# Values by heads copied from SBUF, odd heads' partition halves exchanged, and the output's bank moved

## The chip, the cores and the metric

The kernel runs on one core of one Trainium2 chip. The metric is the time of one execution on the device in microseconds (us); lower is better. Before the change the median of three runs is 4178.27 us (4174.99 to 4178.63).

TensorE (PE in the profile, PEld for its weight loads) multiplies into PSUM, an accumulator memory of eight banks; a bank holds 128 partitions of 512 fp32 values. VectorE (DVE), ScalarE (ACT) and GpSimd (POOL) do the element-wise work. Large data lives in the chip's main memory and comes through SBUF, the on-chip memory, by DMA.

## The reference, cut to what matters

The input is 16 images of 64 x 64 positions with 128 channels. Layer 0 is a two-dimensional LSTM over the grid. Layer 1 is Nystrom attention with 8 heads of 16 channels over the 4096 tokens of an image, followed by a recurrent network. The change is in the attention:

```python
q_l = q.reshape(b, h, m, l, dh).mean(axis=3)      # 64 landmarks
k_l = k.reshape(b, h, m, l, dh).mean(axis=3)
attn1 = softmax(q @ k_l^T);  attn2 = softmax(q_l @ k_l^T);  attn3 = softmax(q_l @ k^T)
out = attn1 @ pinv(attn2) @ (attn3 @ v)
res = conv(v, conv_w)        # 33 taps along the tokens, one filter per head
out = (out + res) @ w_out + b_out
```

What is concerned is `res`, the convolution of the values along the token axis, and the buffers around it. A tile holds 128 tokens, so that a 33-tap filter needs 16 tokens of the tile before and 16 of the tile after.

## The kernel before

The program does group statistics, the LSTM grid, the landmarks and the pseudo-inverse, then `attention` (from about 1760 to 3880 us of the profile's span), then `recurrence`.

In `attention` an image is 32 tiles of 128 tokens, and four tiles make a group of 512 tokens: Q = 8 groups per image, 128 in all. The loop at the end of the function runs 145 steps. A step `s` is `b, q = divmod(s, 8)`, and it works on five groups at once, each at another stage: `new` (group s: queries, keys and values are projected), `mid` (group s-8: weights of the landmarks over the keys), `nxt` (s-15: queries against landmarks, for their maxima), `cur` (s-16: softmax over landmarks and output) and `prev` (s-17: normalisation and the feed to the next layer). Beside them each step does an eighth of the convolution of an earlier image: one pair of heads, over one half (16 tiles) of that image. In the steps q = 0 to 3 it is the second half of image b-2, in q = 4 to 7 the first half of image b-1; 128 such pieces in all.

Inside `tc.manual_schedule` the order on every compute engine is the order of the program text, written out by hand in `step`. The framework puts in the semaphores. It lets no two engines touch one PSUM bank of a tile at the same time, reads included.

PSUM's banks are given by number (`bank(k, shape)`), and a new tile in a bank waits until the readers of the old one have finished. The uses in a step that matter here, in order:

- Banks 0 to 3: `soften(cur)`; then 0, 1, 2 for keys, queries and values in `project(new)`; then 0 to 3 for `greatest(new)`, the key scores of four head pairs, whose maxima DVE takes.
- Banks 4 to 7: `compare(nxt)`, then `weigh(mid)`, then 4 and 5 for `attend(cur)`: the denominators (`gr.den`) and the numerators. Bank 6 then takes `values(mid)` and, later in the step, `output(cur)`. Bank 4 takes the turned convolution in `add_convolved(cur)`. Bank 5 takes `feed(prev)`. Bank 7 takes the convolution.
- `gather(mid)`, once per image at the end of the step q = 7, uses bank 4.

The values of a group come out in bank 2 of `project`. ACT copies them into SBUF (`gr.V`, line 747), and DVE copies them once more out of the same bank into `im.VH`, where they lie by heads (line 749). `im.VH` is what the convolution streams.

`convolve` (line 848) multiplies a head's band matrix, 128 x 128, with the 256 columns (16 tiles x 16 channels) of that head's values: the products inside a tile. `convolve_edges` (line 860) adds the products with the neighbouring tiles. They are small, 32 rows by 32 output tokens: the last 32 tokens of the tile before act on the first 32 of a tile, the first 32 of the tile after on its last 32. Each pair of heads has four of them, all in bank 7. Both heads of a pair use the same rows of TensorE's array: rows 96 to 127 for the one side and 0 to 31 for the other. ACT then copies the bank to `R` (line 864).

In the step q = 3 (`early`) the convolution is done inside `project`, in bank 3 and ahead of the copy at line 749, since that copy writes a tile of `VH` that the convolution of the older image still reads. In all other steps `convolve` stands after `values(mid)` and `convolve_edges` at the end of the step.

`conv_bands` fills the band and edge matrices once, before the loop.

## Time and profile before

| | us |
|---|---|
| median of the runs | 4178.27 |
| profiled execution, its own time | 4171.5 |
| its span, first to last instruction | 4170.0 |
| PE busy | 3949.4 (95%) |
| DVE busy | 2952.6 (71%) |
| POOL busy | 2786.3 (67%) |
| ACT busy | 2521.7 (60%) |
| one image in the middle of `attention` (8 steps) | 125.55 |
| one plain step there | 15.46 |

The profile's page gives each engine's busy time, the chain of work that ended last, and groups of instructions by source line. The timeline lists instructions by start and merges like ones: start, duration of the merged piece, engine, line, operation, names, shape and count, and in square brackets how long the engine stood idle before it and what ended that. An fp32 product of TensorE is two matmul instructions, so counts of matmuls are twice those in the text of the program.

### The profile page before, as it was taken

The numbers are of one execution on the slowest core, as the hardware profiler recorded it, in microseconds if no ns is written. First come the engines' busy times: TensorE is split into PE (matmuls) and PEld (weight loads), VectorE is DVE, ScalarE is ACT, GpSimd is POOL, SyncE is SP. The second block draws the span as 40 slices with busy tenths as digits, with TensorE's granted clock in tenths as the row PEclk, the third lists the DMA queues.
The fourth block names the chain that finished last, engine by engine and source line by source line (L and its number), as shares of the span: only waits on it lengthen the run. The fifth ranks groups of instructions, "written<-read, shape, count | busy, mean of one in ns | idle before, by whom it ended". The sixth has DMA issues, their size and how long they took to land.

```text
span 4170.0 us, 99395 instructions
## 1 busy us (share of the span) xinstructions
PE 3949.4 (95%) x37750; PEld 2661.1 (64%) x37750; DVE 2952.6 (71%) x7136; ACT 2521.7 (60%) x4925; POOL 2786.3 (67%) x4183
## 2 busy tenths in 40 slices
PE   7999999999999979689999999999999999988697
PEld 5857655555676768546666666666666666655386
DVE  8678777777777854346777777777777777757565
ACT  0566655555665643246666766666666666655597
POOL 0677777777777743127788787787787787777133
PEclk9899999999999979899999999999999999989798
DMA  8223322233332200212333333323333323223699
GB/s 330 55 66 82 81 74 78 79 81 82 81 83 73 74 18 4 62 31 61 89 88 83 91 87 84 92 82 89 90 82 89 91 80 91 80 66 86 226 261 182
DMA packets 497778, 386.33 MB, mean 93 GB/s; under 512 B 40464, under 2 KB 470416, under 8 KB 494992
## 3 DMA queue, kind: packets, MB, share of 16 engines
q1 hardware_dynamic: 479888, 346.35, 28.6%
q0 software_dynamic: 17408, 33.56, 4.5%
q8 instruction: 301, 4.93, 0.5%
q14 instruction: 181, 1.48, 0.1%
HBM read 173.74 MB, written 206.18 MB: 91 GB/s over the span
## 4 chain that ended last, share of the span: by engine, by line
PE 85%; DVE 6%; ACT 3%; issue 2%; DMA 2%; POOL 2%; SPq 0%; DVEq 0%; POOLq 0%; ACTq 0%
PE ls_z L194 14%; PE ls_z L198 13%; PE at_bank L737 3%; PE at_bank L775 3%; PE at_bank L848 3%; PE at_bank L860 3%; PE at_bank L982 3%; PE at_bank L809 3%; PE at_bank L745 3%; PE at_bank L930 3%; PE at_bank L954 3%; PE at_bank L740 3%; PE at_bank L887 3%; PE at_bank L920 3%; PE at_bank L824 2%; PE at_bank L721 2%
## 5 line engine op out<-in xcount | busy, mean ns | idle before, releaser
L200 ACT ACTIVATE ls_g<-ls_z,ls_b 128x304 f32<-128x304 f32 (+26 forms) x950 | 509.3, 548 | 369.8 <-PE ls_z L198 333.4
L839 POOL TENSOR_TENSOR at_total<-at_total,at_e 128x512 f32<-128x512 f32 x480 | 612.3, 1276 | 131.5 <-ACT at_e L815 102.6
L194 PE MATMUL ls_z<-ls_xn,ls_w 128*128 128x304 f32 (+26 forms) x1900 | 610.2, 469 | 8.2 <-DMA ls_w<-in_L_conv_wf_dram 5.1
L194 PEld LDWEIGHTS ls_z<-ls_xn,ls_w 128*128 128x128 f32 x1900 | 340.8, 196 | 184.5 <-issue 83.9
L711 POOL TENSOR_SCALAR at_T<-at_T,at_nb 128x128 f32<-128x128 f32 x512 | 405.3, 800 | 13.3
L778 DVE TENSOR_REDUCE at_mxq<-at_bank 128x1 f32<-128x512 f32 x512 | 328.5, 683 | 112.9 <-PE at_bank L775 112.7
L198 PE MATMUL ls_z<-ls_hsum,ls_u 128*128 128x304 f32 (+26 forms) x1140 | 371.1, 462 | 0.0
L280 POOL TENSOR_TENSOR ls_g<-ls_g,ls_cell 128x304 f32<-128x304 f32 (+26 forms) x190 | 176.1, 927 | 277.8 <-ACT ls_g L200 264.8
L894 DVE TENSOR_REDUCE at_cmx<-at_bank 128x8 f32<-128x512 f32 x512 | 317.5, 683 | 58.2 <-PE at_bank L887 57.7
L815 ACT ACTIVATE at_e<-at_bank 128x512 f32<-128x512 f32 x512 | 264.4, 602 | 115.6 <-PE at_bank L809 113.1
L923 ACT ACTIVATE at_eT<-at_bank 128x512 f32<-128x512 f32 x512 | 264.4, 602 | 94.4 <-PE at_bank L920 94.4
L198 PEld LDWEIGHTS ls_z<-ls_hsum,ls_u 128*128 128x128 f32 x1140 | 213.3, 196 | 128.6 <-issue 78.2
L237 ACT ACTIVATE ls_tt<-ls_tt,ls_nb 128x128 f32<-128x128 f32 (+9 forms) x632 | 261.0, 478 | 4.1 <-POOL ls_nb L232 4.1
L198 PE MATMUL ls_z<-ls_h,ls_u 128*128 128x304 f32 (+26 forms) x760 | 259.6, 465 | 2.3 <-DVE ls_h L288 2.0
L228 POOL TENSOR_TENSOR ls_tt<-ls_ve,mhalf 128x4 f32<-128x4 f32 (+2 forms) x190 | 228.6, 1203 | 15.2
L281 DVE TENSOR_TENSOR ls_g<-ls_g,ls_g 128x304 f32<-128x304 f32 (+26 forms) x190 | 98.4, 518 | 194.6 <-POOL ls_g L280 193.4
L1192 DVE SCALAR_TENSOR_TENSOR rc_y<-rc_w,rc_scale,rc_z 128x256 f32<-128x256 f32 x344 | 155.3, 480 | 107.6 <-PE rc_z L1179 99.7
L1179 PE MATMUL rc_z<-rc_y,rc_vT 128*128 128x256 f32 x688 | 187.0, 408 | 39.0 <-ACT rc_y L1200 28.1
L749 DVE COPY at_vh<-at_bank 128x512 f32<-128x512 f32 x128 | 88.5, 692 | 184.4 <-ACT at_v L747 153.1
L975 ACT ACTIVATE at_z<-at_u,at_nb,at_r 128x128 f32<-128x128 f32 x512 | 211.7, 505 | 11.2 <-POOL at_nb L970 11.2
L229 POOL TENSOR_TENSOR ls_tt<-ls_ve,mhalf 128x4 f32<-128x4 f32 (+2 forms) x190 | 214.7, 1130 | 0.0
L985 ACT COPY at_fx<-at_bank 128x512 f32<-128x512 f32 x128 | 132.9, 1038 | 127.1 <-DVE wx_stats L983 101.5
(247 smaller groups left out, 9632.2 us busy)
## 6 DMA issues: line engine op xcount, KB each, us to landing
t<-ls_tt SPq DMA_DIRECT2D x392, 130.0 KB
at_T<-t SPq DMA_DIRECT2D x128, 264.0 KB
gs_xb<-in_x_dram SPq DMA_DIRECT2D x16, 2048.0 KB
at_xh<-t SPq DMA_DIRECT2D x128, 256.0 KB
t<-at_u SPq DMA_DIRECT2D x128, 256.0 KB
out_dram<-at_u SPq DMA_DIRECT2D x128, 256.0 KB
wx<-at_fx SPq DMA_DIRECT2D x128, 256.0 KB
rc_w<-wx SPq DMA_DIRECT2D x64, 512.0 KB
```

The source lines that it names most:

```text
L194: nc.tensor.matmul(v.z[g][:, : v.cols], wt[g], v.xn, start=True, stop=False)
L198: nc.tensor.matmul(view(v, v.z[g]), ut[g], hin, start=False, stop=True)
L200: nc.scalar.activation(a[:, : v.cols], v.z[g][:, : v.cols], AF.Tanh if g == 4 else AF.Sigmoid, bias=bt[g])
L228: nc.gpsimd.tensor_tensor(v.tt[:, 0:k, F + 2], ve[:, 0, :k], mhalf[:, :k], ALU.pow)
L229: nc.gpsimd.tensor_tensor(v.tt[:, 0:k, F + 3], ve[:, 1, :k], mhalf[:, :k], ALU.pow)
L237: nc.scalar.activation(v.tt[:q, k, F + 4 :], v.tt[:q, k, 0:F], AF.Identity, bias=v.nb[:q, k : k + 1], scale=v.tt[:q, k, F + 3 : F + 4],)
L711: nc.gpsimd.tensor_scalar(x[:, c, :], x[:, c, :], gr.nbt[:, 0, c : c + 1], gr.nbt[:, 1, c : c + 1], ALU.mult, ALU.subtract)
L778: nc.vector.tensor_reduce(gr.im.mxq[:, n : n + 1, gr.g], gr.s[n], AX.X, ALU.max)
L815: nc.scalar.activation(gr.e[:, n].rearrange("p c m -> p (c m)"), s[n], AF.Exp)
L839: nc.gpsimd.tensor_tensor(total, total, e[:, :, c, :], ALU.add)
L894: nc.vector.tensor_reduce(gr.mx[:, n].rearrange("p j c -> p c j"), gr.s[n].rearrange("p (c j m) -> p c j m", c=C, j=2), AX.X, ALU.max)
L923: nc.scalar.activation(gr.eT[:, n], s[n], AF.Exp)
```

## The change

- The copy into `VH` (line 749) reads `gr.V` in SBUF and no longer bank 2. It becomes three copies: even heads (128 partitions, 256 elements), and odd heads in two copies of 64 partitions and 256 elements, which exchange the lower and the upper 64 partitions.
- The band and edge matrices of odd heads are filled with their rows exchanged in the same way. So the edge products of an odd head take rows 32 to 63 and 64 to 95, and the four of a pair lie in four different row groups.
- The two heads of a pair go to two banks: bank 7, and the second half of a new bank-6 tile `gr.six`, whose first quarter holds `values`. The addition into `im.sums` becomes `keep_values`, after `convolve`. In the step q = 3 the two banks are 2 and 3.
- The copy to `R` becomes two copies, one per head.
- `output` moves from bank 6 to bank 4; `gather` from bank 4 to bank 5.

```diff
@@ conv_bands
-            nc.vector.tensor_copy(bands[:, h], t[:, 1, :])
-            nc.vector.tensor_copy(edges[P - E :, h], t[P - E :, 0, 0:E])
-            nc.vector.tensor_copy(edges[0:E, h], t[0:E, 2, P - E :])
+            if h % 2 == 0:
+                nc.vector.tensor_copy(bands[:, h], t[:, 1, :])
+                nc.vector.tensor_copy(edges[P - E :, h], t[P - E :, 0, 0:E])
+                nc.vector.tensor_copy(edges[0:E, h], t[0:E, 2, P - E :])
+            else:
+                mid = P // 2
+                nc.vector.tensor_copy(bands[0:mid, h], t[mid:, 1, :])
+                nc.vector.tensor_copy(bands[mid:, h], t[0:mid, 1, :])
+                nc.vector.tensor_copy(edges[mid - E : mid, h], t[P - E :, 0, 0:E])
+                nc.vector.tensor_copy(edges[mid : mid + E, h], t[0:E, 2, P - E :])
@@ project
-            nc.vector.tensor_copy(
-                gr.im.VH[:, :, gr.tiles, :].rearrange("p h k d -> p k h d"), v.rearrange("p (k h d) -> p k h d", k=C, h=H)
-            )
+            to = gr.im.VH[:, :, gr.tiles, :].rearrange("p (n j) k d -> p j k n d", j=2)
+            by = gr.V.rearrange("p k (n j d) -> p j k n d", j=2, d=DH)
+            nc.vector.tensor_copy(to[:, 0], by[:, 0])
+            for rows, other in ((low, high), (high, low)):
+                nc.vector.tensor_copy(to[rows, 1], by[other, 1])
@@ values
-            p = bank(6, [P, P])
+            gr.six = bank(6, [P, 2, 2 * P])
+            p = gr.six[:, 0, 0:P]
...
+        def keep_values(gr):
+            im, p = gr.im, gr.six[:, 0, 0:P]
             if gr.g == 0:
                 nc.vector.tensor_copy(im.sums, p)
             else:
@@ convolve
-            im.cv = bank(k, [P, 2, K // 2, DH])
+            im.cv = [a.rearrange("p (k d) -> p k d", d=DH) for a in of]
...
-                    im.cv[:, j], bands[:, h, :], im.VH[:, h, lo:hi], start=(j == 0), stop=True, skip_group_check=True
+                    im.cv[j], bands[:, h, :], im.VH[:, h, lo:hi], start=True, stop=True, skip_group_check=True
@@ convolve_edges
-                first, last = slice(0, E), slice(P - E, P)
-                for rows, tok, d in ((last, first, -1), (first, last, 1)):
+                for rows, tok, d in ((quarter(3 - 2 * j), quarter(0), -1), (quarter(2 * j), quarter(3), 1)):
...
-            nc.scalar.copy(R[:, lo:hi, 2 * pair : 2 * pair + 2, :].rearrange("p k h d -> p h k d"), im.cv)
+            for j in range(2):
+                nc.scalar.copy(R[:, lo:hi, 2 * pair + j, :], im.cv[j])
@@ gather
-            at = bank(4, [P, C, P])
+            at = bank(5, [P, C, P])
@@ output
-            p = bank(6, [P, C, F])
+            p = bank(4, [P, C, F])
@@ step
-                    convolve(*conv, 3)
+                    convolve(*conv, [a[:, 0 : 2 * P] for a in banks(2, 3)])
...
-                convolve(*conv, 7)
+                convolve(*conv, [bank(7, [P, 2 * P]), mid.six[:, 1] if mid else bank(6, [P, 2 * P])])
+            if mid:
+                keep_values(mid)
```

More of the change, by code (lines that the diff above doesn't have):

```diff
@@ L661, in attention @@
             avs.append(a)
+        low, high = slice(0, P // 2), slice(P // 2, P)
         def quarter(n):
@@ L817, in values @@
         def values(gr):
-            im = gr.im
-            p = bank(6, [P, P])
+            gr.six = bank(6, [P, 2, 2 * P])
+            p = gr.six[:, 0, 0:P]
             for c in range(C):
@@ L839, in add_weights, with convolve @@
                 nc.gpsimd.tensor_tensor(total, total, e[:, :, c, :], ALU.add)
-        def convolve(im, half, pair, k):
+        def convolve(im, half, pair, of):
             lo, hi = half * K // 2, (half + 1) * K // 2
-            im.cv = bank(k, [P, 2, K // 2, DH])
+            im.cv = [a.rearrange("p (k d) -> p k d", d=DH) for a in of]
             for j in range(2):
@@ L856, in convolve_edges @@
                 h = 2 * pair + j
-                first, last = slice(0, E), slice(P - E, P)
-                for rows, tok, d in ((last, first, -1), (first, last, 1)):
+                for rows, tok, d in ((quarter(3 - 2 * j), quarter(0), -1), (quarter(2 * j), quarter(3), 1)):
                     a, z = max(lo, -d), min(hi, K - d)
                     nc.tensor.matmul(
-                        im.cv[tok, j, a - lo : z - lo], edges[rows, h, :], im.VH[rows, h, a + d : z + d],
+                        im.cv[j][tok, a - lo : z - lo], edges[rows, h, :], im.VH[rows, h, a + d : z + d],
                         start=False, stop=True, skip_group_check=True,
                     )
-            nc.scalar.copy(R[:, lo:hi, 2 * pair : 2 * pair + 2, :].rearrange("p k h d -> p h k d"), im.cv)
+            for j in range(2):
+                nc.scalar.copy(R[:, lo:hi, 2 * pair + j, :], im.cv[j])
         def gather(im):
-            at = bank(4, [P, C, P])
+            at = bank(5, [P, C, P])
             nc.tensor.transpose(at[:, 0, :], im.sums, ident)
```

## The prediction

> **What bounds the kernel now.** I read the page first: TensorE is busy 95% of the span, and in the chain that ended last it holds 85%.

> ```profile
> span 4170.0 us, 99395 instructions
> PE 3949.4 (95%) x37750; PEld 2661.1 (64%) x37750; DVE 2952.6 (71%) x7136; ACT 2521.7 (60%) x4925; POOL 2786.3 (67%) x4183
> ```

> Busy is not work done, so next I took the chain in order of time for one plain step (2799.95 to 2815.64; a step lasts 15.46).

> ```profile
> 2804.20 1.30 PE at_bank L775 x6
> ...
> 2812.59 0.98 PE at_bank L860 x7
> 2813.57 0.33 PE at_bank L918 x4
> 2813.89 0.86 PE at_bank L920 x8
> ```

> Two pieces are too long. L920 streams 512 columns for each of four head pairs and takes 0.86. L775 (`greatest`) has the same shape and takes 1.30. L860, the edges, streams four times at most 256 columns, half of L920's, and takes 0.98, more than L920.

> The timeline gives the cause at L775.

> ```profile
> 2803.02 0.59 ACT L747 COPY at_v<-at_bank 128x512 f32<-128x512 f32 x1 [0.29 <-PE at_bank L745]
> 2803.64 0.69 DVE L749 COPY at_vh<-at_bank 128x512 f32<-128x512 f32 x1 [0.95 <-ACT at_v L747]
> 2804.03 1.48 PE L775 MATMUL at_bank<-at_KT,qm 32*128 32x512 f32 x8
> 2804.38 0.30 PEld L775 LDWEIGHTS at_bank<-at_KT,qm 32*128 32x128 f32 x4 [0.15 <-DVE at_vh L749]
> 2805.44 1.07 PE L930 MATMUL at_bank<-at_eT,at_heads 128*32 128x512 f32 x8
> ...
> 2812.51 1.04 ACT L985 COPY at_fx<-at_bank 128x512 f32<-128x512 f32 x1 [0.80 <-DVE wx_stats L983]
> 2812.52 1.05 PE L860 MATMUL at_bank<-at_vh,edges 32*32 32x256 f32 x8
> 2813.62 0.59 ACT L864 COPY at_R<-at_bank 128x512 f32<-128x512 f32 x1
> ...
> 2814.58 1.06 PE L887 MATMUL at_bank<-km,at_QT 32*128 32x128 f32 x32
> ```

> ACT reads bank 2, then DVE; `greatest` wants bank 2 for its third pair and is released at 2804.33. So two pairs run, and two start 0.4 later. The answer for line 775 says how often:

> ```profile
>   DVE at_vh L749: 26.3, 107
> ```

> In the steps q = 0 and q = 3 other products stand between, and L775 is free:

> ```profile
> 2789.00 1.05 PE L775 MATMUL at_bank<-at_KT,qm 32*128 32x512 f32 x8
> 2789.97 1.07 PE L930 MATMUL at_bank<-at_eT,at_heads 128*32 128x512 f32 x8
> ```

> From L775 to L930 it is 0.97 there, 1.41 in the plain step: the wait costs 0.44, though the weight load idles 0.15 only. From L775 to L848 it is 3.70 against 4.14, so the 0.44 survives all that follows.

> [...]
> - [...] DVE's read of bank 2 starts 0.03 after ACT's ends.
> - [...] L920 agrees: four row tiles, four banks, all columns, 0.86 together. [...]
> - [...] a DVE tensor-scalar in SBUF, 128x512, takes 422 ns (L383), the copy from PSUM 692.
> - [...]

> **The change part by part.** All sums are against the span of 4170.0.

> *Copy from SBUF.* Bank 2 is free when ACT ends, 2803.61, and L775's third load wants it at about 2804.03. The wait goes: 107 x 0.44 = 47.1 saved. The DVE copies: 128x128 in SBUF takes 217 (L643), 128x512 422, so 256 elements about 0.285 and three 0.86[...]. They replace 0.69 from 2803.64 and end at 2804.5 to 2804.9; DVE's next work comes at 2805.09. Cost nothing, under DVE's idle 0.76 there. Behind them are the maxima, whose delay reaches TensorE through L941 and L948 only after about 0.3.

> *Four edges together.* L860 issues 8 matmuls, each 256 columns at L920's rate (0.86 for two rounds of 512, so 0.213 for 256). Now they go two at a time, four rounds, 0.85, plus 0.12 around them. Four at a time it is two rounds: saves 0.43 in each of 128 pieces, 54.7. Bounds: 0 if they don't overlap, 0.5 if the switch shrinks too.

> *Two copies to `R`, and bank 6.* This part gives some back. ACT's 128x128 copy takes 266 ns, 128x512 587, so 128x256 about 0.37; two, overlapping by 0.09 as L923's do, 0.66 against 0.59. They stand behind the 1.04 of L985, whose start depends on DVE's L983 and so on L982. In step time with the 0.44 gone, L985 runs 2812.07 to 2813.11 and the second copy (bank 6) ends between 2813.58 and 2813.84. `compare` (L887), moved up by 0.87, loads for bank 6 at about 2813.4 and multiplies there at 2813.8. Delay 0 to 0.25, I take 0.08, since loads run 0.4 ahead: 96 steps (not q = 3 or 7), 7.7 lost, bounds 0 and 24. Queued behind that load are all later products.

> *q = 3.* The convolution now takes bank 2, still being read by ACT:

> ```profile
> 2708.20 1.03 PE L848 MATMUL at_bank<-at_vh,bands 128*128 128x256 f32 x4
> 2708.40 0.59 ACT L747 COPY at_v<-at_bank 128x512 f32<-128x512 f32 x1 [0.29 <-PE at_bank L745]
> ```

> It must wait to 2708.99, with the semaphore and a load (0.15 together): 0.95 of idle TensorE with nothing else in its queue, in 14 steps (images with a `new` group): 13.3 lost.

> *q = 7.* `gather` moves from bank 4, long free, to bank 5, which L985 still reads:

> ```profile
> 2654.41 1.03 ACT L985 COPY at_fx<-at_bank 128x512 f32<-128x512 f32 x1 [0.92 <-DVE wx_stats L983]
> ...
> 2655.28 0.33 PE L869 MATMUL at_bank<-ident,at_sums 128*128 128x128 f32 x1
> ```

> With the 0.44 gone L985 ends at 2655.01; the edges end at 2655.28 - 0.87 = 2654.41. Wait 0.65 with the semaphore, 15 steps: 9.8 lost. Bounds 5 and 13.

> *Costed at nothing.* `keep_values` waits for the convolution's end (2808.9 in the new step) but DVE reaches it at 2809.45. `output` in bank 4 waits for L948, which its own operand waits for anyway. The edges on bank 6 wait for `keep_values`, done two microseconds before. No DMA, and no queue of SP, is touched. If the new waits were exposed, each would cost some 0.1 a step, 13.

> *Rest.* `conv_bands` gets one more copy of 0.29 for four heads, some 1. At q = 3 the three copies meet POOL's 0.80 instructions (L711) and may come 0.2 late, 3.

> Sum: 47.1 + 54.7 - 7.7 - 13.3 - 9.8 - 4.2 = 66.8. The profiled execution is 4171.5, so 4104.7 there. The median of the runs lies 6.8 above it; I take 66.8 off the median: 4178.3 - 66.8 = 4111.5, about 4111.

> **The rivals.**
> 1. *The edges do not overlap four-fold*[...]. For: no row shows it. Against: L920. Then 47.1 - 13.3 - 3 (gather waits 0.2) - 4 = 27 saved: 4151.
> 2. *ACT takes the edges' gain.* If the load of L887 must wait for the second copy to `R` in full, 0.25 or more a step is lost: 24 in place of 7.7, gain 50: 4128. For: the computed times meet within 0.1 us. Against: the second copy may start before L985's end, as L864 does at 2655.39 (L985 ends at 2655.44).
> 3. *Slower: [...]* Place: the three copies after line 747. POOL runs L904, L708, L709 (about 0.2 each) and L711 (2 x 0.80) there. DVE's chain from the maxima on has 0.3 to spare and the net gain is 0.52 a step, so it turns when the copies end 0.8 after 2805.09, at 2805.9[...] Against: POOL's instructions there are mostly short, and only one L711 should be met.
> 4. *The wait at L775 stays*, because ACT's copy or the framework's order still holds bank 2. Then 66.8 - 47.1 = 20 saved: 4158. Against: ACT is done 0.4 before.

> **How the numbers follow.** My forecast 0.70 (own range 4095 to 4125), rival 1 0.10, rival 2 0.10, rival 3 0.06, rival 4 0.02; 0.02 for a mixture that cancels. Best case, both gains whole and none of the waits: 102 saved, 4076. The range 4082 to 4152 takes in the forecast, rivals 1 and 2 and most of the bounds, and leaves out rivals 3 and 4 and the extremes. About 0.2% (8 us) is what this measurement can tell from no change. Faster 0.92, same 0.02, slower 0.06.

> **What the profile after would show.** L775 at 1.05 in every step, and no wait on line 749 before it. L860's piece of the chain near 0.55. Three DVE copies of 256 elements at 0.2 to 0.4 each. Waits for ACT before L848 at q = 3 (0.9), before L869 at q = 7 (0.65), before L887 (0 to 0.25). A plain step of 14.7. The prediction is wrong if L860 stays near 0.98, if DVE stands idle ahead of its three copies while POOL works, or if L887 waits over 0.4.

## The result

The changed kernel takes 4132.76 us, median of five runs (4121.46 to 4135.07), against 4175.58 (4169.72 to 4178.63) for five runs of the kernel before: a ratio of 0.9892, 95% interval 0.9876 to 0.9908. It is 42.8 us faster where 66.8 was forecast. The profiled execution took 4135.07; its span is 4133.6.

The page of the changed kernel, first part:

```profile
span 4133.6 us, 99793 instructions
...
PE 3878.9 (94%) x37750; PEld 2628.1 (64%) x37750; DVE 2983.5 (72%) x7396; ACT 2511.2 (61%) x5053; POOL 2806.8 (68%) x4183
```

The chain on this page reaches back through the last stage only, so I read the timeline. This is a plain step in the middle of the attention (new lines: values copied 757, by heads 761 and 763, key scores 787, edges 874, copies to `R` 879, compare 902):

```profile
2800.42 0.58 ACT L757 COPY at_v<-at_bank 128x512 f32<-128x512 f32 x1 [0.29 <-PE at_bank L755]
...
2801.04 0.39 DVE L761 COPY at_vh<-at_v 128x256 f32<-128x256 f32 x1 [0.97 <-ACT at_v L757]
...
2801.44 1.03 PE L787 MATMUL at_bank<-at_KT,qm 32*128 32x512 f32 x8
2801.44 0.59 DVE L763 COPY at_vh<-at_v 64x256 f32<-64x256 f32 x2
2801.44 0.37 POOL L719 TENSOR_SCALAR at_nb<-at_T 128x4 f32<-128x4 f32 x1
...
2809.47 1.04 ACT L1000 COPY at_fx<-at_bank 128x512 f32<-128x512 f32 x1 [0.80 <-DVE wx_stats L998]
...
2809.47 0.63 PE L874 MATMUL at_bank<-at_vh,edges 32*32 32x256 f32 x8
...
2810.31 0.68 ACT L879 COPY at_R<-at_bank 128x256 f32<-128x256 f32 x2
...
2811.12 1.08 PE L902 MATMUL at_bank<-km,at_QT 32*128 32x128 f32 x32
```

The key scores are down from 1.48 to 1.03 and the edges from 1.05 to 0.63. The step repeats every 14.62 (2801.44 to 2816.06), where it was 15.46: 0.84 of the forecast 0.87 is there. An image takes 121.2 (one piece of edges at q = 4 starts at 2733.57, the next at 2854.77) instead of 125.55. From the first copy at line 985 (now 1000) to the last, which spans nearly the whole attention, it was 1950.0 (1933.6 to 3883.6) and is 1887.1 (1960.2 to 3847.3): 62.9 saved.

So the change does in the steady part what was worked out, and some 20 us go elsewhere: the first copy at that line comes 26.6 later. Of these, the stages before, whose code is the same, ended 5.4 later in this execution (the first product of the bands at 1757.08 and 1751.67), and filling the bands takes 8.9 instead of 7.6. From the end of that to the first copy at line 1000 it is 194.2 (1766.0 to 1960.2) instead of 174.3 (1759.3 to 1933.6). The windows show why. The columns after each stretch are its length, the busy time of PE, PEld, DVE, ACT and POOL with counts, and then the granted TensorE clock, the DMA share and GB/s. The kernel before:

```profile
1780.00:1800.00 20.00, 15.98 (x68) 7.47 (x67) 9.52 (x15) 6.75 (x12) 0.00 (x0) 1.00 0.16 38
1800.00:1820.00 20.00, 16.95 (x66) 7.92 (x64) 8.24 (x13) 6.80 (x11) 0.00 (x0) 0.91 0.11 28
```

The changed kernel, same stretches:

```profile
1780.00:1800.00 20.00, 15.89 (x49) 8.31 (x48) 6.71 (x14) 5.09 (x8) 0.00 (x0) 0.67 0.11 26
1800.00:1820.00 20.00, 15.89 (x49) 8.07 (x49) 6.71 (x14) 5.09 (x8) 0.00 (x0) 0.67 0.10 24
```

TensorE is as busy but works at a granted clock of 0.67, with fewer matmuls in the same time (49 against 68). This is the first image, in which a step has only the `new` group: it projects, multiplies the key scores and takes their maxima. From one copy at line 757 to the next, seven of these eight steps last 10.06 to 10.21 and one 7.39; before, seven lasted 7.06 and one 8.74. In the timeline of the changed kernel:

```profile
1804.12 1.87 PE L787 MATMUL at_bank<-at_KT,qm 32*128 32x512 f32 x8
...
1804.85 0.29 DVE L761 COPY at_vh<-at_v 128x256 f32<-128x256 f32 x1 [6.79 <-ACT at_v L757]
...
1805.16 0.59 DVE L763 COPY at_vh<-at_v 64x256 f32<-64x256 f32 x2
1805.78 2.48 DVE L790 TENSOR_REDUCE at_mxq<-at_bank 128x1 f32<-128x512 f32 x4
...
1807.12 0.80 PE L731 MATMUL at_bank<-ident,at_xh 128*128 128x128 f32 x4 [1.13 <-DVE at_mxq L790]
...
1808.86 2.07 PE L747 MATMUL at_bank<-at_xT,wqkv 128*128 128x512 f32 x2 [0.93 <-ACT at_xT L737]
```

Here nothing covers DVE's three copies. They stand ahead of the maxima; the second maximum frees bank 1, into which the next group's rows are turned (L731), and TensorE waits 1.13 for it and then 0.93 for ACT. Windows of 3.41 us, laid at the changes of the clock, show what it does meanwhile, with the columns as above:

```profile
1800.67:1804.08 3.41, 3.41 (x11) 2.20 (x9) 0.00 (x0) 1.18 (x2) 0.00 (x0) 0.50 0.00 0
1804.08:1807.49 3.41, 2.28 (x12) 0.97 (x12) 2.58 (x6) 0.59 (x1) 0.00 (x0) 1.00 0.00 0
1807.49:1810.90 3.41, 2.48 (x6) 1.06 (x5) 0.77 (x2) 0.78 (x1) 0.00 (x0) 0.50 0.32 77
1810.90:1814.31 3.41, 3.41 (x13) 2.15 (x11) 0.00 (x0) 1.18 (x2) 0.00 (x0) 0.50 0.00 0
```

From 1770 to 1855 of this trace the clock rises eight times, each time after a stretch of 3.41 us in which TensorE was busy throughout (3.41). Here it is full for one such stretch, which holds the key scores and the wait of 1.13, and is back at half when the next projection starts (2.07 for L747, against 1.12 at full clock in a plain step). Three such stretches are 10.24, about as long as the step, so this repeats.

### The profile page after: what moved, and what is told of

Its sections match the earlier page's. It is cut to its first block, busy times and chain, and to the rows that moved or that the text cites. A ratio compares the mean times of both kernels' runs of the same rounds, so it can differ in the third digit from the quotient of the medians.

```text
span 4133.6 us, 99793 instructions
## 1 busy us (share of the span) xinstructions
PE 3878.9 (94%) x37750; PEld 2628.1 (64%) x37750; DVE 2983.5 (72%) x7396; ACT 2511.2 (61%) x5053; POOL 2806.8 (68%) x4183
## 5 line engine op out<-in xcount | busy, mean ns | idle before, releaser
L721 POOL TENSOR_SCALAR at_T<-at_T,at_nb 128x128 f32<-128x128 f32 x512 | 403.7, 796 | 13.3
L1190 POOL DMA_DIRECT2D out_dram<-rc_tt x64 | 77.5, 1212 | 188.1 <-ACT rc_tt L1187 182.1
```

What stands on the lines that cost most here:

```text
L721: nc.gpsimd.tensor_scalar(x[:, c, :], x[:, c, :], gr.nbt[:, 0, c : c + 1], gr.nbt[:, 1, c : c + 1], ALU.mult, ALU.subtract)
```

## The experiments

The theory: the missing 20 us are the low clock of the first eight steps, and it is low because the copies ahead of the maxima raise TensorE's idle share there. The rivals: the longer filling of the bands, the order of the first steps in itself, or chance. Every difference below is against the runs of the kernel before on the same chip.

**One push at the start.** Four products more in the first step of the changed kernel, and the same in the kernel before:

```diff
+            if s == 0:
+                fl = bank(4, [P, GC])
+                for _ in range(4):
+                    nc.tensor.matmul(fl, wqkv[:, 0:P], new.xT, start=True, stop=True)
```

> The changed kernel with four extra products (128x512, into the still unused bank 4) in the first step, to keep TensorE busy for some 3.5 to 7 us longer. Theory (clock): the missing part of the gain is the half clock of the first eight steps of the attention (granted clock 0.59 to 0.79 from 1760 to 1860 us); the filler lets the clock rise once, it then stays, and the kernel gets 15 to 20 us faster than the changed kernel: about 4114, 61 below before. Rival (the first steps are slow for another reason, such as their order or DVE's three copies): nothing is gained, 4133 to 4140, and the clock there stays below 0.8.

> The kernel before with the same four extra products. It has a clock of 0.86 to 1.0 in its first steps, so that both theories expect no gain: 0 to +4 us for the added work. If it gained 10 us or more, the filler would be worth something by itself and would prove nothing on the changed kernel.

Measured: 4136.17 (before 4175.33), no gain, and 4180.98, 5.7 slower than before, a little more than expected. The forecast for the first was a miss, and its windows tell more than its time:

```profile
1780.00:1787.00 7.00, 5.18 (x24) 2.59 (x24) 3.35 (x7) 2.37 (x4) 0.00 (x0) 1.00 0.16 40
1787.00:1800.00 13.00, 10.71 (x28) 5.41 (x29) 3.35 (x7) 3.31 (x6) 0.00 (x0) 0.67 0.16 40
```

The push did bring the clock up, to the full in the second step, and it fell back in the third. So the changed kernel doesn't miss the rise by chance: given the full clock, it did not hold it (0.67 from 1787 to 1840). How much it loses does vary. One of its five runs took 4121.46 with a mean clock of 0.966, the others 4128.78 to 4135.07 with 0.962 or 0.963.

**The copy from SBUF alone**, in the kernel before, as one copy:

```diff
-                ... v.rearrange("p (k h d) -> p k h d", k=C, h=H)
+                ... gr.V.rearrange("p k (h d) -> p k h d", h=H)
```

> The kernel before with one part of the change alone: the values by heads are copied from SBUF (one DVE copy, 128x512), all else as before. By the prediction's term the wait at the key scores goes in 107 steps, 0.44 each: 47 us faster, 4128. If the removed wait is also what leaves the clock low in the first eight steps[...], some 20 of it is lost: 4145 to 4150, with a clock below 0.8 there. If instead the longer filling of the band matrices is what does it, the clock is high here and the gain is the whole 47.

Measured: 4134.65, 40.7 faster, ratio 0.9902 (0.9887 to 0.9918), with a full clock in the first steps (1.00 from 1780 to 1820). The key scores of a plain step take 1.03, and the step 15.02 instead of 15.46. Of the forecast 47 it lacks 6. The trace of the kernel before has 16 of the 107 waits in the first image (two a step, of the weight load and of the product), 7 in the second and 84 after it. In the first image a step gains 0.17 (7.06 to 6.89). In the second it gains nothing (8.90 in both), since there TensorE then waits for ACT, 0.88 before L824 where it was 0.42. So 0.44 holds for 84 waits, 37.0, and with the first image it is 38.4. The step of 8.74 adds 1.7: there the clock of the kernel before was at half for one stretch of 3.41 us.

**The row exchange undone**, all else as changed:

```diff
-            for rows, other in ((low, high), (high, low)):
-                nc.vector.tensor_copy(to[rows, 1], by[other, 1])
+            nc.vector.tensor_copy(to[:, 1], by[:, 1])
@@ convolve_edges
+                for rows, tok, d in ((quarter(3), quarter(0), -1), (quarter(0), quarter(3), 1)):
```

(and `conv_bands` fills all heads as even ones.)

> The changed kernel with the row exchange undone: band and edge matrices and values of odd heads lie as before (two DVE copies, 128x256, in place of three), so that both heads use the same rows and the edges go two at a time, but still in two banks, two copies to R, output in bank 4. The prediction's term: the edges' piece of the chain returns from about 0.55 to 0.98, 0.43 in 128 pieces, 55 us, less what the waits behind it (the load for the compare, gather at q = 7) give back, 0.2 to 0.65 in some steps: 35 to 55 us slower than the changed kernel, 4168 to 4188. Rival (the exchange is worth little, the edges' gain is taken back by ACT's copies): 0 to 20 slower, below 4155.

Measured: 4146.10, 29.2 faster than before and 13.6 slower than the changed kernel. Its edges are back at the old length:

```profile
2724.16 1.05 PE L873 MATMUL at_bank<-at_vh,edges 32*32 32x240 f32 x8
```

The key scores take 1.03 and the early wait is there, so nothing else went back. But its clock in the first steps is full (1.00 from 1780 to 1820). Two copies stand ahead of the maxima there and not three, and TensorE's first wait is 0.63 and not 1.13. The forecast missed because it compared kernels with different clocks. Against the next kernel, with the same clock, the exchange is worth 33.6.

**The copies moved, in the first image only**, behind the fourth maximum:

```diff
+            if gr.im.b > 0:
+                spread(gr)
+
+        def spread(gr):
             to = gr.im.VH[:, :, gr.tiles, :].rearrange("p (n j) k d -> p j k n d", j=2)
@@ step
                 keep_greatest(new, NP - 1)
+                if new.im.b == 0:
+                    spread(new)
```

> The changed kernel with one thing moved: for the first image (the first eight steps) DVE makes the three copies into VH after the fourth maximum and no longer ahead of the first. Theory: in those steps the three copies (0.88) stand ahead of the maxima, whose second frees the bank for the next turned rows; TensorE then idles 1.13 and 0.93 us a step, and at that share the clock falls back to half, also after having been up (in the run with four extra products it was full from 1770 to 1787 us and then fell). Without the copies ahead it idles 0.4 or less and 0.93, the clock stays up, and the kernel is 20 to 26 us faster than the changed kernel: 4107 to 4113, clock 0.97, first steps of 7 us. Rival (the low clock comes from the longer filling of the band matrices or from chance): clock 0.962 and 4128 to 4135.

Measured: 4111.54 (before 4174.37), 62.8 faster, ratio 0.9848 (0.9834 to 0.9862). The eight steps:

```profile
1780.00:1800.00 20.00, 15.32 (x72) 7.94 (x68) 9.71 (x21) 7.51 (x12) 0.00 (x0) 1.00 0.16 40
1800.00:1820.00 20.00, 15.32 (x72) 7.93 (x68) 9.78 (x21) 7.19 (x12) 0.00 (x0) 1.00 0.16 39
```

TensorE's first wait is 0.63, not the 0.4 expected; that was enough. Only in the first step was the clock at half once more, for one stretch (1774.16 to 1777.57). The band filling is as in the changed kernel, so that rival falls.

**The converse.** One and then two copies more ahead of the maxima in the first eight steps of the kernel with the copy from SBUF alone (the edit with two is shown):

```diff
+            if s < Q:
+                scrap = wk.tile([P, GC], F32, tag="z", name="at_scrap")
+                for _ in range(2):
+                    nc.vector.tensor_copy(scrap, new.V.rearrange("p c f -> p (c f)"))
```

> The converse, on the kernel before with only the copy from SBUF (4134.7, clock 0.97 and full in its first steps): one more DVE copy, 128x512 in SBUF (about 0.42 us), is put ahead of the maxima in the first eight steps. Theory: TensorE's idle time per step rises from 0.63 and 0.93 to about 1.05 and 0.93, as in the changed kernel, and the clock stays at half through those steps: 20 to 26 us slower, 4155 to 4161, clock about 0.962. Rival: only the copies themselves are paid, 8 x 0.42 = 3.4 us: 4138.

> As the run with one more DVE copy ahead of the maxima, with two. The first left TensorE idle 0.87 and 0.93 a step, since DVE's copies overlap and start earlier, less than the changed kernel's 1.13 and 0.93, and the clock stayed up. Two copies should bring it to about 1.2 and 0.93. Theory (the share of idle time decides, whatever makes it): the clock stays at half in the first steps, 20 to 26 us slower than with the copy from SBUF alone (4134.7): 4155 to 4161, granted clock near 0.7 from 1780 to 1840. Rival (something else in the changed kernel's first steps, such as its band matrices, keeps the clock low): 4137 to 4141 and a full clock there.

With one copy 4136.71: the forecast 20 to 26 failed. The timeline shows a wait of 0.87 and not the 1.05 that was forecast. The clock fell once in the eight steps, for one stretch of 3.41 us, and came back:

```profile
1783.10 0.66 PE L721 MATMUL at_bank<-ident,at_xh 128*128 128x128 f32 x4 [0.87 <-DVE at_mxq L778]
1784.69 1.13 PE L737 MATMUL at_bank<-at_xT,wqkv 128*128 128x512 f32 x2 [0.93 <-ACT at_xT L727]
```

With two copies 4159.74, 14.3 faster than before in place of 40.7: the second copy of 0.42 cost 23 us. A step that began at full clock, and the windows:

```profile
1803.17 0.66 PE L721 MATMUL at_bank<-ident,at_xh 128*128 128x128 f32 x4 [1.33 <-DVE at_mxq L778]
1804.76 1.13 PE L737 MATMUL at_bank<-at_xT,wqkv 128*128 128x512 f32 x2 [0.93 <-ACT at_xT L727]
```

```profile
1780.00:1800.00 20.00, 15.49 (x50) 8.04 (x46) 7.16 (x14) 4.64 (x8) 0.00 (x0) 0.66 0.11 27
1800.00:1820.00 20.00, 14.18 (x57) 6.99 (x56) 9.59 (x20) 5.68 (x9) 0.00 (x0) 0.91 0.11 26
1820.00:1840.00 20.00, 16.14 (x48) 8.43 (x48) 6.50 (x14) 5.10 (x8) 0.00 (x0) 0.66 0.10 27
```

This kernel has neither the exchanged rows nor the other bands. With a first wait of 1.33 in place of 0.87 the clock was low (0.66, 0.91 and 0.66) without them.

**The wait filled.** The changed kernel with DVE's order untouched and one product more per step in the first image:

```diff
+                if s < Q:
+                    nc.tensor.matmul(bank(4, [P, GC]), wqkv[:, 0:P], new.xT, start=True, stop=True)
```

> The changed kernel, DVE's order untouched, with one extra product (128x512, into the unused bank 4) in each of the first eight steps, after the key scores, where TensorE waits for DVE. [...] Theory (it is TensorE's idle share): the clock goes up and holds, 18 to 24 us faster than the changed kernel: 4109 to 4115. Rival (DVE's late maxima matter in themselves): 4130 to 4136, clock 0.962.

Measured: 4115.49 (before 4174.03), 58.5 faster, with the clock at 1.00 (windows, and the added product in the timeline):

```profile
1780.00:1800.00 20.00, 17.01 (x69) 7.77 (x66) 10.06 (x21) 6.05 (x11) 0.00 (x0) 1.00 0.16 39
```

```profile
1803.34 1.12 PE L1054 MATMUL at_bank<-at_xT,wqkv 128*128 128x512 f32 x2
```

DVE's order is that of the changed kernel, and a step takes 7.39, as long as the one step in which the changed kernel kept its full clock. So neither the late maxima nor the length of the step decides. In these runs the low clock went with TensorE's idle time: 0.67 with first waits of 1.13, 0.66 to 0.91 with 1.33 that other copies caused, and 1.00 where the product of 1.12 filled the wait.

**The two new waits.** The prediction gave 13.3 us to the wait of the early convolution and 9.8 to that of `gather`. Both are there in the changed kernel:

```profile
2778.63 0.33 PE L884 MATMUL at_bank<-ident,at_sums 128*128 128x128 f32 x1 [0.56 <-ACT at_fx L1000]
...
2830.30 1.13 PE L862 MATMUL at_bank<-at_vh,bands 128*128 128x256 f32 x4 [0.68 <-ACT at_v L757]
```

On top of the moved copies, first other banks for the one, then for the other as well:

```diff
-                    convolve(*conv, [a[:, 0 : 2 * P] for a in banks(2, 3)])
+                    convolve(*conv, [a[:, 0 : 2 * P] for a in banks(3, 1)])
@@ gather
-            at = bank(5, [P, C, P])
+            at = bank(4, [P, C, P])
```

> The kernel with the copies moved in the first image, and the early convolution in banks 3 and 1 in place of 2 and 3. The prediction put the wait for ACT's copy out of bank 2 at 0.95 in 14 steps. Bank 1 is free by then, so the wait goes: 10 to 14 us faster than the kernel with the copies moved alone. Rival (the wait only stands in place of one that comes later in the step): 0 to 4.

> Both of the former, and gather back in bank 4. The prediction put gather's wait for ACT's last read of bank 5 at 0.65 in 15 steps. Bank 4 is released by DVE's addition of the output, about 0.3 earlier: 4 to 6 us faster than the kernel with banks 3 and 1. In all 36 to 46 below the changed kernel: about 4092.

Measured: 4100.93 with banks 3 and 1, 10.6 less; in the traces the step q = 3 goes from 16.05 to 15.11. Then 4093.17 with `gather` in bank 4 too, another 7.8. The second is more than the wait that went, 0.28 in 15 steps, or 4. In the timeline of this last kernel gather waits 0.28 and the early convolution not at all:

```profile
2739.00 0.33 PE L888 MATMUL at_bank<-ident,at_sums 128*128 128x128 f32 x1 [0.28 <-DVE at_u L975]
...
2789.83 1.03 PE L866 MATMUL at_bank<-at_vh,bands 128*128 128x256 f32 x4
```

The rest lies within the spread of the runs (4095.38 to 4110.01 and 4089.63 to 4097.45). With all three edits the kernel is 81.2 faster than before, ratio 0.9809 (0.9795 to 0.9822), and 38 faster than the change as it came.

## Why the prediction was right, and where it was not

- *Direction and range*: faster, and 4132.8 lies within 4082 to 4152, but outside the forecast's own 4095 to 4125.
- *Copy from SBUF*, 47.1: alone it gave 40.7. The mechanism was right (1.48 to 1.03 in the steps named). The size was off because 0.44 was multiplied with all 107 waits. Only 84 of them lie after the first two images, in which the maxima or ACT set the pace.
- *Three copies costed at nothing, "under DVE's idle 0.76 there"*: this is the step that failed. The cover was read from a plain step and used for all 128. In the first image there is no cover, and the three copies hold the maxima up. At full clock that is 0.5 a step (7.38 in the run with the push, 6.89 with the copies moved), 4 us in eight steps. With the clock, of which the prediction says nothing, it is 20.0: 62.8 saved with the copies moved, 42.8 without.
- *Edges*, 54.7 before the waits: a piece went from 1.05 to 0.63, 0.42 in 128 pieces, 53.8. In the traces without and with the exchange (rows undone, and copies moved) a plain step goes from 15.02 to 14.62, and the step q = 7 stays at 16.28, where the wait of `gather` takes the gain. That is 0.40 in seven of eight pieces, some 45. The medians of these runs differ by 33.6. Of the 11 between, 3.6 lie in the first two images, in which the run with the exchange had two stretches of half clock more; the rest is not traced, and the two medians have spreads of 7 and 9.
- *Compare held up by the copies to `R`*, 7.7: the weight load waits 14.1 us in 85 places, but TensorE only once, 0.5, since the loads run ahead (by 0.43 in the plain step, L902); that step lacks only 0.03. Rival 2 did not happen.
- *q = 3*, 13.3: TensorE idles 0.68 and its product is 0.1 longer. Undone, the step is 0.94 shorter, which is 13.2 in 14 steps and just the term; the medians show 10.6. *q = 7*, 9.8: 8.5 of idle TensorE in 15 places.
- *Rival 3*, DVE's copies and POOL's instructions holding each other up: something of the kind is in the plain step above, L761 at 0.39 instead of 0.29 and POOL's L719 at 0.37 instead of 0.23 (L709 before). In all 85 places where L719 meets a copy of line 763 it takes 0.36 to 0.38, in the 43 others 0.22 or 0.23. A tenth or so each, not the 1.4 that it needed (the copies' end at 2805.9, less 2803.64 and their own 0.86).
- *Rivals 1 and 4* fell with the durations of L874 and L787.

With the first image put right, the kernel takes 4111.5, the predicted time. That is partly luck: the copy's term was 6 too large, the exchange gave less than the edges' term, the compare's loss of 7.7 did not come, and the forecast counted from 4178.3, where the kernel before took 4174.4 beside this run.

## What to carry to other kernels

A cost hidden under an engine's idle time is hidden only in the steps where that idle time exists: look at the first steps of a software pipeline, where most stages are empty, before multiplying a plain step's sum. In the first image, where TensorE waits twice a step, a few tenths of a microsecond more of waiting went with the loss of its full clock: with two added copies ahead of the maxima and not one the first wait was 1.33 and not 0.87, the clock from 1780 to 1800 was 0.66 and not 1.00, and the kernel was 23 us slower. So check the granted clock by windows in each stretch of a changed kernel, and put work that nobody waits for behind the work that frees a buffer.

## What the runs showed of the hardware that was not expected

Where the edge lies is not shown. In the windows of the changed kernel the clock falls after a stretch with 2.28 us of busy TensorE, 67%. In the kernel with one more copy it holds after 1.93 (57%) and falls after 1.63 (48%):

```profile
1789.68:1793.09 3.41, 1.93 (x7) 1.09 (x8) 1.69 (x3) 0.89 (x2) 0.00 (x0) 1.00 0.31 73
1793.10:1796.51 3.41, 3.40 (x18) 1.65 (x16) 1.16 (x3) 1.65 (x3) 0.00 (x0) 1.00 0.01 4
1796.51:1799.92 3.41, 1.63 (x7) 0.92 (x8) 1.99 (x4) 0.78 (x1) 0.00 (x0) 1.00 0.20 48
1799.92:1803.33 3.41, 3.41 (x11) 2.25 (x9) 0.00 (x0) 1.18 (x2) 0.00 (x0) 0.50 0.10 29
```

So in these runs the busy share of the last stretch does not decide by itself. After 1799.92 the clock was at half for a wholly busy stretch and rose again, and was not lost a second time in these steps.

The clock fell after stretches in which TensorE was busy for 2.28 and 1.63 of 3.41, so it did not take a wholly idle one. And a step about as long as three such stretches (10.24) settled into a rhythm: in the changed kernel's first image each of the seven full-clock stretches after which it fell holds a wait of 1.12 or 1.13, and seven of eight steps took 10.06 to 10.21 instead of 7.06.
